# Pairwise bilinear products: a fixed issue order, units of one PSUM bank and a third product three units later

## Chip, core and metric

The kernel runs on one core of a Trainium2 chip. The metric is device time in microseconds, the median of several runs. The kernel before took 898.36 us (three runs, 897.13 to 898.63). A profiled execution of it spans 896.0 us.

## The reference

There are 32 fields of 128 numbers for each of 1024 rows, and one 128 x 128 matrix for each of the 496 pairs of fields. For each pair (i, j) with i < j, field i is multiplied by the pair's matrix, and the result element by element by field j, all in float32:

```python
FIELD_SIZE, EMBED_SIZE = 32, 128
_pairs = np.array(list(itertools.combinations(range(FIELD_SIZE), 2)))
v_i = inputs[:, I_IDX, :]            # inputs: (1024, 32, 128)
v_j = inputs[:, J_IDX, :]
transformed = jnp.einsum('bpd,ped->bpe', v_i, W)   # W: (496, 128, 128)
return transformed * v_j             # (1024, 496, 128)
```

The output has 1024 x 496 x 128 float32 numbers, 260 MB, and is much larger than the inputs.

## The kernel before

The host transposes the inputs, so that a field is a tile `x` of 128 x 1024 (embedding by rows of the batch) and the matrices come in chunks of four (`WC = 4`). Pairs are taken with falling i, so the first fields have few pairs: i = 30 has one, i = 29 two, and so on.

The first 15 pairs (`nq0`, "native") are multiplied as they are, in float32. For all others, each factor is split into three parts in a faster 32-bit format (float32r): `h` holds the leading part, `l` the rest, `d` a difference of the two. Then the product is the sum of three matrix products, where the sum of the first two is scaled by 1 + 2^-12 before the third is added:

```python
EPS = 2.0**-12
NATIVE = 5
LAG = 2
...
    def split_w(c):
        ...
        nc.scalar.mul(h, raw, 1.0 - 2.0**-13)                               # ACT
        nc.gpsimd.tensor_tensor(l, raw, h.bitcast(F32), ALU.subtract)       # POOL
        nc.gpsimd.tensor_scalar(hs, h.bitcast(F32), EPS, 1.0, ALU.mult, ALU.mult)
        nc.gpsimd.tensor_tensor(d, l.bitcast(F32), hs, ALU.subtract)
```

A field is split in the same way, in two halves of 512 columns. The main loop goes over whole pairs. Each pair has one PSUM tile `po` of 128 x 1024, two banks, of which there are four:

```python
    for q in range(NQ + LAG):
        if q < NQ:
            ...                       # loads; split of the chunk two ahead, split of the next field
            po[q] = ppool.tile([P, BT], F32, tag="po", name=f"po_{q}")
            ...
                for t in (0, 1):                        # first two products, L170
                    for h in range(0, BT, HB):
                        nc.tensor.matmul(po[q][:, h : h + HB], w_s[c][t][:, r],
                                         x_s[i][t][:, h : h + HB], start=t == 0, stop=t == 1)
                nc.scalar.mul(po[q], po[q], 1.0 + EPS)  # scaling in place, L177
        if q >= LAG:
            if q - LAG >= nq0:
                second(q - LAG)                         # third product, two matmuls, L135
            finish(q - LAG)                             # times field j (VectorE, L128), store
```

The kernel is written in a framework whose scheduler may put the instructions of an engine in another order than that of the source; here it is left to do so. All loads and stores are issued from SyncE's queue. Output tiles `ot` are 128 x 1024, six of them.

Of the kernel before, what the change touches and what calls it, by code (L numbers as in the profile page):

```python
# [1 line left out]

# [4 lines left out]

F32 = mybir.dt.float32
F32R = mybir.dt.float32r
ALU = mybir.AluOpType  # L10

P = 128
NF = 32
NQ = NF * (NF - 1) // 2
BT = 1024
HB = 512
WC = 4
EPS = 2.0**-12
NATIVE = 5
LAG = 2  # L20


def _pairs():

    return [(i, j) for i in range(NF - 2, -1, -1) for j in range(i + 1, NF)]


@with_exitstack
def kernel(
    ctx: ExitStack,  # L30
    tc: tile.TileContext,
    xt: bass.AP,
    wt: bass.AP,
    out: bass.AP,
):

    nc = tc.nc
    pairs = _pairs()
    nchunk = NQ // WC

    xpool = ctx.enter_context(tc.tile_pool(name="x", bufs=1))
    spool = ctx.enter_context(tc.tile_pool(name="xs", bufs=2))
    rpool = ctx.enter_context(tc.tile_pool(name="wr", bufs=4))
    wpool = ctx.enter_context(tc.tile_pool(name="ws", bufs=3))
    tpool = ctx.enter_context(tc.tile_pool(name="tmp", bufs=2))  # L60
    opool = ctx.enter_context(tc.tile_pool(name="o", bufs=6))
    ppool = ctx.enter_context(tc.tile_pool(name="ps", bufs=4, space=bass.MemoryType.PSUM))

    x_sb = {}

    def load_x(f, pieces=1):
        x_sb[f] = xpool.tile([P, BT], F32, tag=f"x{f}", name=f"x_{f}")
        s = BT // pieces
        for k in range(pieces):
            nc.sync.dma_start(out=x_sb[f][:, k * s : (k + 1) * s], in_=xt[:, f, k * s : (k + 1) * s])  # L70

    w_raw = {}

    def load_w(c, splits=(0, WC)):
        w_raw[c] = rpool.tile([P, WC, P], F32, tag="w", name=f"w_{c}")
        for a, b in zip(splits, splits[1:]):
            nc.sync.dma_start(out=w_raw[c][:, a:b, :], in_=wt[:, c * WC + a : c * WC + b, :])

    w_s = {}

    def split_w(c):

        raw = w_raw[c].rearrange("p q e -> p (q e)")
        h, l, d = [wpool.tile([P, WC * P], F32R, tag=t, name=f"{t}_{c}") for t in ("wh", "wl", "wd")]
        hs = tpool.tile([P, WC * P], F32, tag="t", name=f"whs_{c}")
        nc.scalar.mul(h, raw, 1.0 - 2.0**-13)  # L86
        nc.gpsimd.tensor_tensor(l, raw, h.bitcast(F32), ALU.subtract)  # L87
        nc.gpsimd.tensor_scalar(hs, h.bitcast(F32), EPS, 1.0, ALU.mult, ALU.mult)  # L88
        nc.gpsimd.tensor_tensor(d, l.bitcast(F32), hs, ALU.subtract)  # L89
        w_s[c] = (h, l, d)  # L90

    x_s = {}

    def split_x(f):

        h, l, d = [spool.tile([P, BT], F32R, tag=t, name=f"{t}_{f}") for t in ("xh", "xl", "xd")]
        for a in range(0, BT, HB):
            s = slice(a, a + HB)
            ls = tpool.tile([P, HB], F32, tag="t", name=f"xls_{f}_{a}")
            nc.scalar.mul(h[:, s], x_sb[f][:, s], 1.0 - 2.0**-13)  # L100
            nc.gpsimd.tensor_tensor(ls, x_sb[f][:, s], h[:, s].bitcast(F32), ALU.subtract)  # L101
            nc.gpsimd.tensor_scalar(l[:, s], ls, 1.0 / EPS, 1.0, ALU.mult, ALU.mult)  # L102
            nc.gpsimd.tensor_tensor(d[:, s], h[:, s].bitcast(F32), l[:, s].bitcast(F32), ALU.subtract)  # L103
        x_s[f] = (h, l, d)

    nq0 = NATIVE * (NATIVE + 1) // 2
    c0 = nq0 // WC

    load_w(0, (0, 1, WC))
    load_x(NF - 2, 2)  # L110
    load_x(NF - 1, 2)
    load_x(NF - 3)
    load_w(1)
    for f in (NF - 4, NF - 5):
        load_x(f)
    load_w(2)

    out_v = out.rearrange("q e b -> q e b")
    po = {}

    def finish(q):
        j = pairs[q][1]
        ot = opool.tile([P, BT], F32, tag="ot", name=f"ot_{q}")
        pieces = 2 if q >= NQ - 2 else 1
        s0 = BT // pieces
        for k in range(pieces):
            s = slice(k * s0, (k + 1) * s0)
            nc.vector.tensor_tensor(ot[:, s], po[q][:, s], x_sb[j][:, s], ALU.mult)  # L128
            nc.sync.dma_start(out=out_v[q, :, s], in_=ot[:, s])

    def second(q):
        i, _ = pairs[q]
        r = slice(q % WC * P, (q % WC + 1) * P)
        for h in range(0, BT, HB):
            nc.tensor.matmul(  # L135
                po[q][:, h : h + HB], w_s[q // WC][2][:, r], x_s[i][2][:, h : h + HB], start=False, stop=True,
                skip_group_check=True,
            )

    for q in range(NQ + LAG):  # L140
        if q < NQ:
            i, j = pairs[q]
            c = q // WC
            if q % WC == 0:
                if c + 3 < nchunk:
                    load_w(c + 3)
                for k in ([c + 2] if c > 0 else [0, 1, 2]):
                    if c0 <= k < nchunk:
                        split_w(k)
            if j == i + 1:  # L150
                for f in ([i - 4] if i < NF - 2 else [NF - 6]):
                    if f >= 0:
                        load_x(f)
                if 0 <= i - 1 < NF - 1 - NATIVE:
                    split_x(i - 1)
            po[q] = ppool.tile([P, BT], F32, tag="po", name=f"po_{q}")
            if q < nq0:
                for h in range(0, BT, HB):
                    nc.tensor.matmul(  # L159
                        po[q][:, h : h + HB],  # L160
                        w_raw[c][:, q % WC, :],
                        x_sb[i][:, h : h + HB],
                        start=True,
                        stop=True,
                    )
            else:
                r = slice(q % WC * P, (q % WC + 1) * P)
                for t in (0, 1):
                    for h in range(0, BT, HB):
                        nc.tensor.matmul(  # L170
                            po[q][:, h : h + HB],
                            w_s[c][t][:, r],
                            x_s[i][t][:, h : h + HB],
                            start=t == 0,
                            stop=t == 1,
                        )
                nc.scalar.mul(po[q], po[q], 1.0 + EPS)  # L177
        if q >= LAG:
            if q - LAG >= nq0:
                second(q - LAG)  # L180
            finish(q - LAG)


# [25 lines left out]
```

## Time and profile before

| Part | Value |
|---|---|
| Median time | 898.36 us |
| Span of the profiled execution | 896.0 us |
| Bytes moved | 310.03 MB, of them 260.05 MB written to HBM |
| VectorE multiply, 128 x 1024 (L128), 494 times | 1224 ns each |
| VectorE multiply, 128 x 512, 4 times | 685 ns each |
| ACT scaling in PSUM, 128 x 1024 (L177), 481 times | 1009 ns each |
| ACT split of a weight chunk, 128 x 512 (L86), 121 times | 624 ns each |
| GpSimd, one split of a chunk (L87, L88, L89) | 1277, 621 and 1294 ns |
| GpSimd, busy in all | 549.5 us |
| Matmuls of 512 columns, L170 and L135 | 4 and 2 for each split pair |
| Store of 512 KB, issue to landing | 3.8 us median |

PE is the matrix engine, PEld its weight loads (which overlap it), DVE is VectorE, ACT ScalarE, POOL GpSimd, SP SyncE. "L177" is line 177 of the kernel. In the page's busy shares, 100% would be an engine that never stands still. A matmul's recorded length is longer than the step from one to the next, since they are pipelined, so the steps between starts in the timeline say more. In a list of waits each line names who waited, for whom, how long in all, how often and the longest single wait.

### The profile page before, as it was taken

Reading aid. Unit: us, or ns where it says so; the run is one execution under the profiler, and the core shown is the slowest. Engines: PE = TensorE matmul, PEld = TensorE weight load, DVE = VectorE, ACT = ScalarE, POOL = GpSimd, SP = SyncE. Lnnn points to the kernel's source line nnn. Section 1 sums busy time; section 2 is a strip of 40 time slices with the busy share of each in tenths; the row PEclk is TensorE's granted clock in tenths of the full one; section 3 lists DMA queues with packets and bytes.
Section 4 is the critical chain, followed back from the end, with each engine's and each line's share of the span. In section 5 each row is a group of like instructions: output and inputs, shape, how many; then the busy total and the mean of one; then the engine's idle time right before and its main releaser. Section 6 shows DMA issues by size and latency. Waiting matters only on the chain.

```text
span 896.0 us, 10407 instructions
## 1 busy us (share of the span) xinstructions
PE 761.1 (85%) x2946; PEld 526.2 (59%) x2946; DVE 607.0 (68%) x498; ACT 558.2 (62%) x655; POOL 549.5 (61%) x523
## 2 busy tenths in 40 slices
PE   7988888888888888888888888888888888898887
PEld 2455555555666565555565666655656566665665
DVE  3666666666777666676676767776667777677766
ACT  2266666666676566566665667665756666666565
POOL 1878877777666774664747565665655647474441
PEclk9999999999999999999999999999999999999999
DMA  8999999899999898998998999998998899999997
GB/s 329 416 340 370 360 355 343 318 361 338 376 357 362 332 370 327 339 361 320 353 343 336 343 363 356 355 352 321 355 341 334 336 339 330 343 345 339 337 342 304
DMA packets 94666, 310.03 MB, mean 346 GB/s; under 512 B 10513, under 2 KB 10769, under 8 KB 94609
## 3 DMA queue, kind: packets, MB, share of 16 engines
q1 hardware_dynamic: 94608, 309.37, 92.3%
q8 instruction: 23, 0.38, 0.2%
q14 instruction: 35, 0.28, 0.1%
HBM read 49.28 MB, written 260.05 MB: 345 GB/s over the span
## 4 chain that ended last, share of the span: by engine, by line
PE 32%; ACT 25%; issue 19%; POOL 11%; DMA 1%; DVE 0%; POOLq 0%; ACTq 0%; DVEq 0%
ACT po L177 20%; PE po L170 17%; PE po L135 14%; ACT wh L86 4%; POOL wl L87 4%; POOL wd L89 4%; POOL whs L88 2%; DMA out_dram<-ot 1%; ACT xh L100 1%; POOL xls L101 1%; DVE ot L128 0%; POOL xl L102 0%; POOLq L87 0%; ACTq L177 0%; POOL xd L103 0%
## 5 line engine op out<-in xcount | busy, mean ns | idle before, releaser
L128 DVE TENSOR_TENSOR ot<-po,x 128x1024 f32<-128x1024 f32 (+1 forms) x498 | 607.0, 1220 | 285.4 <-ACT po L177 141.7
L177 ACT ACTIVATE po<-po 128x1024 f32<-128x1024 f32 x481 | 476.9, 1009 | 298.5 <-PE po L170 298.5
L135 PE MATMUL po<-xd,wd 128*128 128x512 f32 x962 | 325.7, 420 | 123.8 <-ACT po L177 123.0
L87 POOL TENSOR_TENSOR wl<-w,wh 128x512 fp32r<-128x512 f32 x121 | 154.5, 1277 | 301.7 <-ACT wh L86 301.7
L135 PEld LDWEIGHTS po<-xd,wd 128*128 128x128 f32 x962 | 152.7, 188 | 257.5 <-ACT po L177 162.8
L170 PE MATMUL po<-xh,wh 128*128 128x512 f32 x962 | 300.9, 394 | 0.0
L170 PE MATMUL po<-xl,wl 128*128 128x512 f32 x962 | 298.1, 391 | 0.0
L170 PEld LDWEIGHTS po<-xl,wl 128*128 128x128 f32 x962 | 180.6, 188 | 42.2
L170 PEld LDWEIGHTS po<-xh,wh 128*128 128x128 f32 x962 | 180.6, 188 | 42.1 <-issue 0.5
L89 POOL TENSOR_TENSOR wd<-wl,whs 128x512 fp32r<-128x512 f32 x121 | 156.6, 1294 | 7.9
L86 ACT ACTIVATE wh<-w 128x512 fp32r<-128x512 f32 x121 | 75.5, 624 | 19.3 <-DMA w<-in_wt_dram 19.3
L88 POOL TENSOR_SCALAR whs<-wh 128x512 f32<-128x512 f32 x121 | 75.1, 621 | 10.2
L101 POOL TENSOR_TENSOR xls<-x,xh 128x512 f32<-128x512 f32 x52 | 67.4, 1296 | 4.2
L103 POOL TENSOR_TENSOR xd<-xh,xl 128x512 fp32r<-128x512 f32 x52 | 66.9, 1287 | 2.2
L100 ACT ACTIVATE xh<-x 128x512 fp32r<-128x512 f32 x52 | 32.1, 621 | 13.6 <-PE po L170 8.7
L102 POOL TENSOR_SCALAR xl<-xls 128x512 fp32r<-128x512 f32 x52 | 32.4, 623 | 4.4
L159 PE MATMUL po<-x,w 128*128 128x512 f32 x60 | 29.6, 656 | 6.2 <-DMA x<-in_xt_dram 6.2
L159 PEld LDWEIGHTS po<-x,w 128*128 128x128 f32 x60 | 12.3, 209 | 22.6 <-issue 21.6
L86 ACT ACT_TABLE_LOAD x1 | 1.3, 1283 | 0.7 <-PEq L196 0.7
L196 POOL MEMSET const-float32-0.0<- 128x1 f32 x1 | 0.1, 99 | 0.2 <-issue 0.2
L196 POOL MEMSET const-bfloat16-1.0<- 128x1 bf16 x1 | 0.1, 102 | 0.0
L196 POOL MEMSET const-uint8-127<- 128x1 uint8 x1 | 0.1, 102 | 0.0
(1 smaller groups left out, 0.1 us busy)
## 6 DMA issues: line engine op xcount, KB each, us to landing
out_dram<-ot SPq DMA_DIRECT2D x494, 512.0 KB, 3.8
w<-in_wt_dram SPq DMA_DIRECT2D x123, 256.0 KB, 3.9
x<-in_xt_dram SPq DMA_DIRECT2D x30, 512.0 KB, 6.0
x<-in_xt_dram SPq DMA_DIRECT2D x4, 256.0 KB, 4.4
out_dram<-ot SPq DMA_DIRECT2D x4, 256.0 KB, 2.6
w<-in_wt_dram SPq DMA_DIRECT2D x1, 192.0 KB, 2.6
w<-in_wt_dram SPq DMA_DIRECT2D x1, 64.0 KB, 1.8
```

Source lines behind the costliest of these rows:

```text
L86: nc.scalar.mul(h, raw, 1.0 - 2.0**-13)
L87: nc.gpsimd.tensor_tensor(l, raw, h.bitcast(F32), ALU.subtract)
L88: nc.gpsimd.tensor_scalar(hs, h.bitcast(F32), EPS, 1.0, ALU.mult, ALU.mult)
L89: nc.gpsimd.tensor_tensor(d, l.bitcast(F32), hs, ALU.subtract)
L100: nc.scalar.mul(h[:, s], x_sb[f][:, s], 1.0 - 2.0**-13)
L101: nc.gpsimd.tensor_tensor(ls, x_sb[f][:, s], h[:, s].bitcast(F32), ALU.subtract)
L103: nc.gpsimd.tensor_tensor(d[:, s], h[:, s].bitcast(F32), l[:, s].bitcast(F32), ALU.subtract)
L128: nc.vector.tensor_tensor(ot[:, s], po[q][:, s], x_sb[j][:, s], ALU.mult)
L135: nc.tensor.matmul(po[q][:, h : h + HB], w_s[q // WC][2][:, r], x_s[i][2][:, h : h + HB], start=False, stop=True, skip_group_check=True,)
L159: nc.tensor.matmul(po[q][:, h : h + HB], w_raw[c][:, q % WC, :], x_sb[i][:, h : h + HB], start=True, stop=True,)
L170: nc.tensor.matmul(po[q][:, h : h + HB], w_s[c][t][:, r], x_s[i][t][:, h : h + HB], start=t == 0, stop=t == 1,)
L177: nc.scalar.mul(po[q], po[q], 1.0 + EPS)
```

## The change

The loop now goes over units of half a pair: 512 columns, one PSUM bank, eight such tiles instead of four of two banks. For each unit there are two matmuls, the scaling, and, three units later, the third product and the multiply. The third product thus stands three units behind its scaling, and this order is the one each engine gets: `tc.manual_schedule()` has the instructions issued as they are written. The splits go into a list with an earliest place and a deadline, and at most one is dealt out behind each pair, the most urgent first; a field's split is dealt out in two halves. Besides this, weight chunks are loaded four ahead instead of three (five tiles instead of four), output tiles go from six to five, and the first two fields are loaded from ScalarE's queue instead of SyncE's. The sizes of matmuls, splits and stores stay; scaling and multiply become twice as many of half the size. The aim is that the engines no longer wait for one another within a pair.

The core of the diff, with cuts marked:

```diff
-LAG = 2
+LAG = 3
+WLEAD = 4
+XLEAD = 3
...
-    rpool = ctx.enter_context(tc.tile_pool(name="wr", bufs=4))
+    rpool = ctx.enter_context(tc.tile_pool(name="wr", bufs=5))
...
-    opool = ctx.enter_context(tc.tile_pool(name="o", bufs=6))
-    ppool = ctx.enter_context(tc.tile_pool(name="ps", bufs=4, space=bass.MemoryType.PSUM))
+    opool = ctx.enter_context(tc.tile_pool(name="o", bufs=5))
+    ppool = ctx.enter_context(tc.tile_pool(name="ps", bufs=8, space=bass.MemoryType.PSUM))
...
+    todo = []
+    for c in range(c0, nchunk):
+        todo.append(((c - 2) * WC + 1, max(c * WC, nq0), lambda c=c: split_w(c)))
+    for i in range(NF - 2 - NATIVE, -1, -1):
+        for a in range(0, BT, HB):
+            todo.append((first_q[i + 1] + 1 if i < NF - 3 - NATIVE else 2, first_q[i], lambda i=i, a=a: split_x(i, a)))
+    todo.sort(key=lambda t: t[1])
...
-    load_x(NF - 2, 2)
-    load_x(NF - 1, 2)
+    load_x(NF - 2, 2, nc.scalar)
+    load_x(NF - 1, 2, nc.scalar)
...
+    ctx.enter_context(tc.manual_schedule())
...
+    def first(u):
+        q, h = divmod(u, 2)
+        ...
+        po[u] = ppool.tile([P, HB], F32, tag="po", name=f"po_{u}")
+        if q < nq0:
+            nc.tensor.matmul(po[u], w_raw[c][:, q % WC, :], x_sb[i][:, s], start=True, stop=True)
+        else:
+            for t in (0, 1):
+                nc.tensor.matmul(po[u], w_s[c][t][:, r], x_s[i][t][:, s], start=t == 0, stop=t == 1)
+            nc.scalar.mul(po[u], po[u], 1.0 + EPS)
+
+    def second(u):
+        ...
+        if q >= nq0:
+            nc.tensor.matmul(
+                po[u], w_s[q // WC][2][:, r], x_s[i][2][:, s], start=False, stop=True, skip_group_check=True
+            )
+        if h == 0:
+            ots[q] = opool.tile([P, BT], F32, tag="ot", name=f"ot_{q}")
+        nc.vector.tensor_tensor(ots[q][:, s], po.pop(u), x_sb[j][:, s], ALU.mult)
+        if q >= NQ - 2:
+            nc.sync.dma_start(out=out[q, :, s], in_=ots[q][:, s])
+        elif h == 1:
+            nc.sync.dma_start(out=out[q], in_=ots[q])
+
+    for u in range(2 * NQ + LAG):
+        q = u // 2
+        if u % (2 * WC) == 0 and q // WC + WLEAD < nchunk:
+            load_w(q // WC + WLEAD)
+        if u < 2 * NQ:
+            ...
+            first(u)
+        if u >= LAG:
+            second(u - LAG)
+        if u % 2 == 1:
+            ready = [t for t in todo if t[0] <= q]
+            if ready:
+                ready[0][2]()
+                todo.remove(ready[0])
```

## Prediction

> **What bounds the kernel now.** I began with busy shares, to see whether any engine is full, and with the transfers beside them (first and third part of the page, and the DMA rows of the slices).
>
> ```profile
> PE 761.1 (85%) x2946; PEld 526.2 (59%) x2946; DVE 607.0 (68%) x498; ACT 558.2 (62%) x655; POOL 549.5 (61%) x523
> DMA  8999999899999898998998999998998899999997
> GB/s 329 416 340 370 360 355 343 318 361 338 376 357 362 332 370 327 339 361 320 353 343 336 343 363 356 355 352 321 355 341 334 336 339 330 343 345 339 337 342 304
> ...
> q1 hardware_dynamic: 94608, 309.37, 92.3%
> ```
>
> No engine is full, yet the DMA engines look nearly so, at 346 GB/s on average. Two things say that they are not the limit. One slice moved 416 GB/s. And the view of the DMA queue's waits has its stores waiting for VectorE ("SPq L129 <- DVE ot L128: 574.6"), while in the view of the engines' waits no store delays VectorE. I then asked for short windows. The columns are: length, busy time and count of PE, PEld, DVE, ACT and POOL, clock, DMA share, GB/s.
>
> ```profile
> 16.00:46.00 30.00, 28.27 (x80) 14.52 (x79) 20.46 (x18) 8.95 (x12) 22.98 (x24) 1.00 1.03 417
> 400.00:428.00 28.00, 24.11 (x95) 16.49 (x95) 18.42 (x16) 18.80 (x23) 14.59 (x15) 1.00 0.88 322
> 429.00:444.00 15.00, 12.30 (x50) 8.49 (x48) 10.48 (x9) 8.71 (x10) 13.28 (x13) 1.00 1.03 407
> 410.00:412.00 2.00, 2.00 (x10) 1.45 (x9) 1.85 (x2) 1.51 (x3) 0.00 (x0) 1.00 0.27 109
> ```
>
> Where work is always queued, DMA sustains 407 to 417 GB/s; in between it runs dry (410 to 412 us: 27%, 109 GB/s). So the stores wait for the computation. Next, who waits there (engine and line, releaser, total us, times, longest):
>
> ```profile
> ACT po L177 <- PE po L170: 298.5, 237, 7.8
> PEld po L135 <- ACT po L177: 162.8, 195, 1.7
> DVE ot L128 <- ACT po L177: 141.7, 89, 1.6
> PE po L135 <- ACT po L177: 123.0, 245, 1.2
> DVE ot L128 <- PE po L135: 114.7, 347, 1.7
> ```
>
> PE and ACT wait for each other. The timeline shows the form (start, length, engine, operation, idle before it):
>
> ```profile
> 403.26 0.62 PE L170 MATMUL po<-xh,wh 128*128 128x512 f32 x2
> 403.72 0.61 PE L170 MATMUL po<-xl,wl 128*128 128x512 f32 x2
> 404.52 0.73 PE L135 MATMUL po<-xd,wd 128*128 128x512 f32 x2 [0.19 <-ACT po L177]
> 405.97 0.74 PE L135 MATMUL po<-xd,wd 128*128 128x512 f32 x2 [0.72 <-ACT po L177]
> ```
> ```profile
> 403.46 1.01 ACT L177 ACTIVATE po<-po 128x1024 f32<-128x1024 f32 x1 [1.75 <-PE po L170]
> 404.38 0.62 ACT L86 ACTIVATE wh<-w 128x512 fp32r<-128x512 f32 x1
> 404.91 1.02 ACT L177 ACTIVATE po<-po 128x1024 f32<-128x1024 f32 x1
> ...
> 411.41 0.62 ACT L86 ACTIVATE wh<-w 128x512 fp32r<-128x512 f32 x1
> ```
>
> PE issues the first two products of two pairs back to back. ACT scales the first pair from 403.46 to 404.47, and PE's third product starts at 404.52, right behind it. ACT then splits a weight chunk before it scales the second pair, and PE stands another 0.72 us. The scheduler has put the pairs so that the lag of two written in the source is hardly there. The chunk splits recur every 411.41 - 404.38 = 7.03 us, which is 4 pairs: **1.76 us per pair**. Over the whole body I get the same: VectorE's product of pair 15 ends near 37 us (timeline), the last near 892, so (892 - 37) / 481 = 1.78 us.
>
> **What the Trainium skill says.** "PSUM — Partial Sum Buffer", section "PSUM bank collisions raise a hardware error", has engines kept apart bank by bank. A tile of two banks is therefore handed over as a whole, as the trace has it: one ACT instruction of 1024 columns, and both third products behind it. "Perfetto Trace Analysis", section "Optimizing Scalar/DVE Operations", says that larger operations help a saturated engine, while breaking them up can help where an engine that is not saturated causes bubbles in others; ACT at 62% with 123.0 us of PE waiting is that case. It puts the cost of one more instruction on PSUM at about 125 ns for DVE and 51 ns for ScalarE; the trace agrees roughly for DVE (146 ns of recorded time, below). "TensorE: Matmul & The Clock Gate", section "Back-to-back issue gap", has N/2.4 + 2.5 ns, so 216 ns for 512 columns; here two take 403.72 - 403.26 = 0.46 us, 230 ns each. "HBM Reference", section "Specifications (TRN2)", has about 425 GB/s for a core that streams alone; 417 was measured here.
>
> **The change part by part**, per pair, the 481 split pairs first.
>
> - **PE.** The same six matmuls: 6 x 0.23 = 1.38 us. A third product comes three half-pair units later. A unit is 0.69 us of PE work, and between the first two products of u and its third lie the third products of u-3, u-2 and u-1 and the first two of u+1, u+2 and u+3: 9 matmuls, 2.07 us. The scaling needs about 0.6, or 1.2 with a split ahead of it. So the 123.0 us of waiting should nearly vanish; alone this would make 896 - 123 = 773.
> - **ACT.** 962 scalings of 512 columns for 481 of 1024. No such row exists. It must cost over half of 1009 ns, and at most the 624 ns of the 512-column split: 1.01 to 1.25 us per pair, plus (75.5 + 32.1) / 481 = 0.22 of splits, so 1.23 to 1.47. Two consecutive 1024s take 1.93 us and not 2.02, as records overlap; I take 1.3.
> - **VectorE.** 992 halves for 498. The four halves at the end took 685 ns each, so 1.37 us per pair against 1.22, 73 us more in sum, with nothing of it on the path while below PE.
> - **GpSimd.** 549.5 / 481 = 1.14 us, unchanged. One split takes 1277 + 621 + 1294 = 3.19 us. For a field of n pairs it needs 2 + n/4 splits, 6.4 + 0.8n. With 1.5n available, it is late only for n of 6, 7 and 8: about 2, 1.5 and 1 us. A cost of up to 5 us.
> - **PSUM.** Eight tiles of one bank are the same memory as four of two. A unit lives through two matmuls, scaling, third product and multiply, some 4 units; 8 are there.
> - **Transfers.** The same 310.03 MB. Output tiles fall from 6 to 5. One is filled in 1.4 us and landed 3.8 us after issue, so 5.2 us of holding is covered by 5 x 1.5 = 7.5 us. First loads of two fields go out from ACT's queue; under 1 us. Looking further ahead in loads costs nothing.
> - **The first 15 pairs** have one matmul per half, with PE nearly full (28.27 of 30 us). They stay: 37 us to the end of pair 15.
>
> So computation can run at 1.4 us per pair, and **the transfers become the bound**: 310.03 MB / 0.407 to 0.417 = 743 to 762 us, plus about 2 us until the first loads and 4 for the last store, 750 to 768. They won't be perfectly full, since computation has only some 8% in hand over the 310.03 / 496 / 0.412 = 1.52 us of a pair. Every time a cluster of splits or a boundary lets the queue run dry, full speed is lost for a moment. I allow 25 to 35 us, which means a mean of about 392 GB/s: 791, plus 2 to 3 us between the span and the given time (898.36 against 896.0). **794 us.**
>
> **Rivals.**
>
> - **A. The transfers are the bound already.** For it: nines in nearly every slice. 309.37 MB at a 92.3% share is 374 GB/s when busy, which would give 310.03 / 0.374 + 6 = 835 us. Against it: 407 and 417 GB/s in full stretches. I chose the upper rate because the low rates stand beside dry spells; that rests on a few stretches, so 835 stays in my range.
> - **B. The fixed order makes new stalls.** No engine can now step past a late input, and a split on ACT stands ahead of scalings. For it: splits come in threes where a field starts. Against it: the third product has near 0.9 to 1.4 us to spare, and 8 banks. Half the PE waiting kept would give 896 - 62 = 834 or so.
> - **C. Smaller instructions make ACT or VectorE the bound.** If ACT took 624 ns, 1.47 us x 481 + 37 + 5 = 749, still under the transfers. It could only make them less full.
> - **D. Slower.** It would need more than 1.80 us per pair. No engine's sum is near it.
>
> **Range and chances.** The lower end is the full rate, 768. The upper end is A or B alone, 835. Over 880 would need both at once. So 768 to 836, with 0.95 for faster by over 2%, 0.04 for within, 0.01 for slower.
>
> **What the profile after would show.** Right: PE's wait for ACT at the third product near zero; a mean of 385 GB/s or more, with slices over 400 in the middle; VectorE halves of about 685 ns and a VectorE share over 80%; waits of VectorE or its output tile for stores appearing, since stores now lag. Wrong by A: DMA share near 1.0 with 375 GB/s. Wrong by B: PE or VectorE still idle behind ACT or GpSimd, and dry spells of DMA. Wrong on ACT: scalings of 512 columns over 624 ns.

## The result and the profile after

The changed kernel takes **780.49 us** (779.83 to 781.02) against 898.5: a ratio of 0.869, 95% interval 0.867 to 0.870. The prediction was 794, with a range of 768 to 836. A profiled execution spans 779.2 us. First the page's busy shares, the slices' rows of DMA, its queue, and the shares of the chain that ended last:

```profile
PE 725.1 (93%) x2946; PEld 544.4 (70%) x2946; DVE 632.7 (81%) x992; ACT 622.3 (80%) x1136; POOL 549.9 (71%) x523
DMA  9899999999999999999999999999999999999998
GB/s 341 352 397 399 411 403 400 405 399 411 395 411 403 399 401 412 401 399 407 394 408 410 399 390 388 411 408 410 397 403 401 392 403 403 404 393 407 402 408 341
...
q1 hardware_dynamic: 94032, 308.32, 100.3%
...
DMA 42%; PE 31%; DVE 12%; POOL 8%; issue 4%; SPq 1%; DVEq 0%; POOLq 0%
```

Away from the edges the same bytes now flow at 388 to 412 GB/s in each slice; in the kernel before it was 318 to 376. Transfers lead the chain with 42%, of which stores are 41%. Before, the same line read:

```profile
PE 32%; ACT 25%; issue 19%; POOL 11%; DMA 1%; DVE 0%; POOLq 0%; ACTq 0%; DVEq 0%
```

The window that held the dry spells before (columns as in the prediction), and the whole of the body:

```profile
400.00:428.00 28.00, 26.82 (x112) 20.42 (x111) 23.91 (x38) 23.55 (x44) 20.89 (x20) 1.00 1.02 407
46.00:770.00 724.00, 686.25 (x2844) 525.28 (x2845) 606.28 (x951) 607.90 (x1112) 524.66 (x495) 1.00 1.02 403
```

The waits have turned round:

```profile
PEld po L147 <- DVE ot L161: 93.2, 135, 2.5
...
DVE ot L161 <- DMA out_dram<-ot: 67.7, 75, 3.2
DVE ot L161 <- PE po L156: 44.8, 60, 1.9
...
PEld po L156 <- ACT po L148: 0.4, 1, 0.4
```

At the third product PE had waited 123.0 us for the scaling and its weight load 162.8 us; PE's wait is gone and the weight load's is 0.4 us. Instead VectorE waits for output tiles that stores still hold (67.7), and PE for PSUM that VectorE holds (34.2, its weight load 93.2). The delay comes from the stores backwards, where it came from PE and ACT forwards. That the queue of stores waits for VectorE tells nothing by itself: it did so for 574.6 us before, and still does for 365.8 us ("SPq L165 <- DVE ot L161: 365.8"). VectorE's wait for stores is what is new. The timeline of PE shows the pace in between:

```profile
400.01 0.39 PE L147 MATMUL po<-xl,wl 128*128 128x512 f32 x1
400.23 0.39 PE L156 MATMUL po<-xd,wd 128*128 128x512 f32 x1
400.46 0.40 PE L147 MATMUL po<-xh,wh 128*128 128x512 f32 x1
400.70 0.40 PE L147 MATMUL po<-xl,wl 128*128 128x512 f32 x1
400.93 0.40 PE L156 MATMUL po<-xd,wd 128*128 128x512 f32 x1
```

In this stretch a third product starts every 400.93 - 400.23 = 0.70 us without a gap. Two rows of part 5 give the halved instructions:

```profile
L161 DVE TENSOR_TENSOR ot<-po,x 128x512 f32<-128x512 f32 x992 | 632.7, 686 | 140.7 <-DMA out_dram<-ot 67.7
L148 ACT ACTIVATE po<-po 128x512 f32<-128x512 f32 x962 | 544.4, 580 | 130.1 <-PE po L147 77.3
```

### The profile page after: what moved, and what is told of

Same layout as the page of the kernel before. It is cut to its first block, busy times and chain, and to the rows that moved or that the text cites. A ratio compares the mean times of both kernels' runs of the same rounds, so it can differ in the third digit from the quotient of the medians.

```text
span 779.2 us, 11845 instructions
## 1 busy us (share of the span) xinstructions
PE 725.1 (93%) x2946; PEld 544.4 (70%) x2946; DVE 632.7 (81%) x992; ACT 622.3 (80%) x1136; POOL 549.9 (71%) x523
## 2 busy tenths in 40 slices
DMA packets 94676, 310.12 MB, mean 398 GB/s; under 512 B 10512, under 2 KB 10768, under 8 KB 94608
## 4 chain that ended last, share of the span: by engine, by line
DMA 42%; PE 31%; DVE 12%; POOL 8%; issue 4%; SPq 1%; DVEq 0%; POOLq 0%
DMA out_dram<-ot 41%; PE po L147 22%; DVE ot L161 12%; PE po L156 10%; POOL wd L91 2%; POOL wl L89 2%; POOL whs L90 1%; POOL xls L104 1%; DMA x<-in_xt_dram 1%; DMA w<-in_wt_dram 1%; SPq L79 1%; SPq L165 0%; POOL xd L106 0%; POOL xl L105 0%; DVEq L161 0%
## 5 line engine op out<-in xcount | busy, mean ns | idle before, releaser
L161 DVE TENSOR_TENSOR ot<-po,x 128x512 f32<-128x512 f32 x992 | 632.7, 686 | 140.7 <-DMA out_dram<-ot 67.7
L148 ACT ACTIVATE po<-po 128x512 f32<-128x512 f32 x962 | 544.4, 580 | 130.1 <-PE po L147 77.3
L147 PE MATMUL po<-xh,wh 128*128 128x512 f32 x962 | 391.5, 407 | 39.5 <-DVE ot L161 34.2
L147 PE MATMUL po<-xl,wl 128*128 128x512 f32 x962 | 377.8, 393 | 1.5 <-POOL wl L89 1.5
L156 PE MATMUL po<-xd,wd 128*128 128x512 f32 x962 | 377.3, 393 | 0.0
L147 PEld LDWEIGHTS po<-xh,wh 128*128 128x128 f32 x962 | 181.0, 188 | 133.6 <-DVE ot L161 93.2
L89 POOL TENSOR_TENSOR wl<-w,wh 128x512 fp32r<-128x512 f32 x121 | 156.1, 1290 | 156.3 <-ACT wh L88 153.8
L156 PEld LDWEIGHTS po<-xd,wd 128*128 128x128 f32 x962 | 181.2, 188 | 40.3 <-ACT po L148 0.4
L103 ACT ACTIVATE xh<-x 128x512 fp32r<-128x512 f32 x52 | 32.6, 629 | 13.6 <-DMA x<-in_xt_dram 13.5
```

Source lines behind the costliest of these rows:

```text
L103: nc.scalar.mul(h, x_sb[f][:, s], 1.0 - 2.0**-13)
L147: nc.tensor.matmul(po[u], w_s[c][t][:, r], x_s[i][t][:, s], start=t == 0, stop=t == 1)
L148: nc.scalar.mul(po[u], po[u], 1.0 + EPS)
L156: nc.tensor.matmul(po[u], w_s[q // WC][2][:, r], x_s[i][2][:, s], start=False, stop=True, skip_group_check=True)
L161: nc.vector.tensor_tensor(ots[q][:, s], po.pop(u), x_sb[j][:, s], ALU.mult)
```

## The experiments

The change does three things at once: it fixes the order, halves the units, and deals the splits out. I took them apart, then asked what bounds the result. For the reading it helps to count, in the compiled order of PE's instructions, how many matmuls lie between a unit's first two products and its third. Those matmuls are all that the scaling has to hide behind. (The trace does not number the tiles; third products are taken in the order of their units.)

```
kernel           unit      matmuls between (times)              in us at 0.23 each
before           pair      0 (11), 2 (114), 4 (114), 6 (242)    0 to 1.38
changed          half      9 (956 of 962)                       2.07
free_order       half      1 (129), 2 (139), 3 (679), other 15  mostly 0.69
before_fixed     pair      12 (477 of 481)                      2.76
```

The source of the kernel before says two pairs, which would be 12. No third product got that.

### The order alone, and the small units alone

before_fixed is the kernel before with one line more; free_order is the changed kernel with that line out:

```diff
 # before_fixed (in the kernel before)
+    ctx.enter_context(tc.manual_schedule())
 # free_order (in the changed kernel)
-    ctx.enter_context(tc.manual_schedule())
```

The letters in the expectations from here on are not those of the prediction: O is the theory that the fixed order brings the gain, B that units of one bank do, S that dealing out the splits does.

> The kernel before with its order fixed as written and nothing else: whole pairs, two banks, third product two pairs later, splits in clumps at the start of a chunk and of a field. Theory O: 785 to 815 us, PE waiting for ACT at the third product under 20 us, DMA near 400 GB/s. Rival B (one-bank units): 860 us or more. Rival S (splits must be dealt out): 830 to 870 us, with PE behind ACT or GpSimd where splits come in clumps.

Measured: **783.08 us**, ratio 0.872 (0.870 to 0.874). One line gives nearly all of the gain, with clumped splits and whole pairs left as they were. The page and the waits:

```profile
PE 763.0 (98%) x2946; PEld 517.8 (66%) x2946; DVE 607.4 (78%) x498; ACT 563.3 (72%) x655; POOL 550.4 (70%) x523
...
DMA packets 94665, 310.03 MB, mean 396 GB/s; under 512 B 10512, under 2 KB 10768, under 8 KB 94608
```
```profile
PEld po L171 <- DVE ot L129: 127.3, 410, 0.4
...
PE po L136 <- ACT po L178: 5.3, 9, 1.6
```

The third product's wait for ACT is 5.3 us. What is left is the weight load of PE waiting about 0.3 us in most pairs for VectorE to give back a tile of two banks. Rivals B and S both fall, as far as the total time goes.

> The changed kernel without the line that fixes the order; the scheduler then puts the third product one unit behind its first two for 818 of 962 units and directly behind for 134. Theory O (the fixed order, which keeps the third product far behind the scaling, brings the gain): most of the gain is lost, 830 to 890 us, PE waiting for ACT at the third product more than 80 us. Rival B (units of one bank bring the gain, since halves are handed over sooner): 780 to 800 us, hardly any such wait.

Measured: **960.96 us**, ratio 1.071 (1.068 to 1.073): half-pair units and dealt splits, in an order of the scheduler's choosing, are slower than the kernel before. It is also above the 830 to 890 us that were expected. The waits, the largest first:

```profile
PEld po L155 <- ACT po L147: 365.2, 812, 1.1
...
ACT po L147 <- PE po L146: 266.2, 442, 10.4
DVE ot L160 <- PE po L155: 250.5, 580, 1.6
PE po L155 <- ACT po L147: 82.6, 269, 0.7
```

PE's weight load for the third product waits 812 times for the scaling. Halved units halve the distance that one unit of lag is worth. The distances account for most of the time: lag1 below, with 3 matmuls between for nearly every unit, takes 847 us, and here 129 units have two matmuls less (0.46 us) and 139 one less (0.23 us), which gives 847 + 59 + 32 = 938 of the 961 us. This is an estimate made after the runs.

### How far apart is enough

Next the distance was set, with the order fixed. First in half-pair units, LAG = 1 and LAG = 2 instead of 3:

> The changed kernel with the third product one unit later instead of three. Between the first two products and the third of a unit lie 3 matmuls, 0.69 us; the scaling needs 0.58 us and a split ahead of it another 0.62. Theory O: each of 173 splits delays PE by about 0.6 us and scaling by itself is just at the edge, so 810 to 860 us. Rival (distance does not matter once order is fixed and units are one bank): 780 to 785 us.

Measured: 846.67 us, ratio 0.943 (0.941 to 0.945), as theory O had it. The wait for the scaling at the third product is back:

```profile
PEld po L156 <- ACT po L148: 192.7, 579, 0.5
```

> The third product two units later. 6 matmuls, 1.38 us, against 1.2 us of scaling with one split ahead. Theory O: 780 to 785 us, as for three, since one split is just covered and small delays are hidden behind the transfers. Rival (every unit of distance counts): 790 to 820 us.

Measured: 778.21 us, ratio 0.867 (0.865 to 0.869), within 0.3% of three units. 1.38 us of distance covers scaling and one split (0.58 + 0.62 = 1.20); the weight load's wait for the scaling is 3.4 us, in 15 places.

Then in whole pairs, LAG = 1 and LAG = 0 in before_fixed:

> The kernel before with fixed order and the third product one whole pair later. In the order that the scheduler gave the kernel before, 356 third products stand one pair later and 125 directly behind their own first two. Theory Z (the products without distance are what cost): between first and third products lie 6 matmuls, 1.38 us, against 1.01 of scaling, so only the splits in clumps hurt, 785 to 820 us. Rival (one pair is already too near, the scheduler's other choices included): 870 us or more.

Measured: 803.60 us, ratio 0.897 (0.894 to 0.899), as theory Z had it; this leaves out a fourth run, of 818.21 us, in which the granted clock was 0.977 instead of 0.989 to 0.993.

```profile
ACT wh L86 <- DMA w<-in_wt_dram: 82.5, 61, 12.2
...
PE po L136 <- ACT po L178: 61.1, 74, 3.2
```

Here the wait is not that of the lengths added up in the expectation. In 61 places ACT, whose order is fixed too, stands at the split of a weight chunk that has not landed, with a scaling behind it; 54.0 of PE's 61.1 us follow such a place within 3.5 us. The changed kernel loads chunks four ahead instead of three, and ACT waits 2.1 us for them. In before_fixed ACT waits even longer for them, 129.6 us, but the 12 matmuls between hide it.

> The same with no distance: the third product directly behind its pair's first two. Theory Z: each pair takes 4 matmuls, the scaling and 2 matmuls one after the other, 0.92 + 1.01 + about 0.1 + 0.46 = 2.5 us, so 1180 to 1260 us. A mix of 356 pairs at the pace of whole_lag1 and 125 at this pace should then give the kernel before within 25 us of its 898. Rival: the mix misses by more than 50 us.

Measured: 1373.97 us, ratio 1.533 (1.530 to 1.536); I had expected at most 1260.

```profile
DVE ot L129 <- PE po L136: 742.9, 480, 1.8
...
PE po L136 <- ACT po L178: 538.9, 481, 1.4
```

PE waits at each of 481 pairs, 538.9 / 481 = 1.12 us, and VectorE waits in turn for PE's late products.

The mix that I had expected misses: 804 + 125/481 x (1374 - 804) = 952 against 898. That is 54 us off, beyond the 25 us of theory Z and also beyond the 50 us from which the rival was to hold. The count above shows one reason. I had counted 125 pairs of the kernel before as having no distance, but 114 of them have another pair's third product in between, 0.46 us. Putting 1.12 us on 11 pairs, 0.66 on 114, and 0.20 on the 114 with four matmuls gives 12 + 75 + 23 = 110, so 804 + 110 = 914. That is within 2% of 898, but it was worked out after the result, and the rest stays open. That whole_lag0 is 0.27 us per pair slower than my sum can be read from its trace, as a mean over the 481 pairs: 1.12 us from a pair's first matmul to the start of its scaling where I had put 0.92, since the scaling starts 0.43 us after the start of the last of the four matmuls and not one step of 0.23; 1.01 for the scaling; 0.08 until the third product; and 0.57 from there to the next pair where I had put 0.46. Together 2.78 us. The trend over all runs is clear in one table:

```
matmuls between    0      3 (halves)   6 (halves)   6 (pairs)   9 (halves)   12 (pairs)
us              1374        847           778          804         780          783
```

At six, pairs cost more than halves. A pair's scaling takes 1.01 us of the 1.38 and a half's 0.58, so a split ahead of it (0.62) fits only with halves; but the waits of whole_lag1 show that most of its loss comes from the late weight chunks.

### Dealing the splits out

```diff
-            if ready:
-                ready[0][2]()
-                todo.remove(ready[0])
+            if q % WC == 1:
+                for t in ready:
+                    t[2]()
+                    todo.remove(t)
```

> The changed kernel with all splits that are ready issued at once behind the second pair of each chunk, instead of one behind each pair. Three splits in a row put 1.87 us ahead of the scaling, against 1.4 us of spare distance, at each of 25 fields; theory O: under 1 us of PE waiting per clump, hidden behind transfers, so 778 to 792 us. Rival S (dealing out is needed): 800 us or more, with PE waiting for ACT at the third product over 25 us.

Measured: 777.84 us, ratio 0.866 (0.865 to 0.868). PE's weight load waits 4.8 us for the scaling, in 12 places. Dealing out brings nothing here. This version is even some 2 us faster than the changed kernel (777.84, 776.26 to 778.35, against 779.71, 779.60 to 781.44, on the same chip); the reason shows below, at early_split.

### What bounds it now

half_store stores half of the columns and computes all; half_store_before does the same in before_fixed; no_third leaves the third product out, and with it a third of PE's work on those pairs:

```diff
 # half_store
-            nc.sync.dma_start(out=out[q], in_=ots[q])
+            nc.sync.dma_start(out=out[q, :, :HB], in_=ots[q][:, :HB])
 # no_third
-        if q >= nq0:
+        if q < 0:
             nc.tensor.matmul(po[u], w_s[q // WC][2][:, r], ...
```

> The changed kernel storing only the first 512 of 1024 columns of each pair (half of the output is left unwritten; all is still computed), 180 MB instead of 310. Theory T (the transfers bound the changed kernel): the time falls to what PE needs, 36 us to the first split pair and 962 units of 0.69 us, so 700 to 730 us. Rival (computation still bounds it): 770 us or more.

Measured: 706.22 us, ratio 0.787 (0.785 to 0.789). PE and VectorE are now nearly full (page, part 1):

```profile
PE 686.4 (97%) x2946; PEld 553.8 (79%) x2946; DVE 671.3 (95%) x992; ACT 613.6 (87%) x1136; POOL 551.4 (78%) x523
```

> The changed kernel without the third product (left out, so the sum lacks its last part); PE has 4 matmuls per pair instead of 6, 219 us less of work. Theory T (transfers bound): 770 to 783 us, nothing or little gained. Rival (PE bounds): 700 us or less.

Measured: 775.04 us, ratio 0.863 (0.861 to 0.865). With 219 us less PE work the kernel gains some 5 us, while half of the store bytes were worth 74. So **the transfers bound the changed kernel**, with only a small share for PE.

> The kernel before with fixed order, storing half of the columns as in half_store. It shows what the one-bank units are worth once transfers no longer hide it. With four tiles of two banks a tile comes free only after a multiply of 1.22 us that starts when both third products are done, about 1.45 us after the slot in which the next user wants it begins to count down from 1.38 us; I expect 1.46 to 1.55 us per pair, so 740 to 785 us, against 700 to 730 for the changed kernel. Rival (one-bank units bring nothing even in computation): within 1% of half_store.

Measured: 771.54 us, ratio 0.860 (0.858 to 0.861). Here is what the small units do:

```profile
PE 758.9 (99%) x2946; PEld 518.5 (67%) x2946; DVE 607.4 (79%) x498; ACT 574.2 (75%) x655; POOL 551.5 (72%) x523
```
```profile
PEld po L172 <- DVE ot L129: 131.1, 432, 0.4
```

With half of the stores gone, before_fixed becomes only 12 us shorter, since PE's weight load waits 0.3 us for a two-bank tile in 432 pairs whatever the stores do; the changed kernel becomes 74 us shorter, and in half_store the same wait is nearly gone:

```profile
PEld po L147 <- DVE ot L161: 2.7, 3, 1.2
```

The changed kernel's structure is thus worth 771.54 - 706.22 = 65 us of computation, or (769.5 - 37) / 481 = 1.52 us per pair against (704.2 - 36) / 481 = 1.39, and the transfers hide it nearly all. The two also differ in dealing, loads ahead and output tiles, but the only long wait of PE that goes away is the one for two-bank tiles. By its recorded PE share before_fixed looks fuller than the changed kernel (98% against 93%). A matmul's record, 395 ns in the median there, is longer than the step of 230 ns, so short pauses between starts don't show as idle time.

### A version that beats both

In the changed kernel DMA has one dry spell of about 3 us, near the first split pairs. The timeline around it (GpSimd's first split, then the chunk that the second split pair needs, and PE):

```profile
18.10 1.27 POOL L104 TENSOR_TENSOR xls<-x,xh 128x512 f32<-128x512 f32 x1 [17.66 <-ACT xh L103]
...
34.55 1.26 POOL L89 TENSOR_TENSOR wl<-w,wh 128x512 fp32r<-128x512 f32 x1
...
35.87 0.50 PE L147 MATMUL po<-xl,wl 128*128 128x512 f32 x1 [1.51 <-POOL wl L89]
```

PE stands at the first products of the second split pair until their chunk is split, with the third products of the first pair queued behind them. GpSimd works without a pause from 18.10 us on; it starts so late because its first split is of a field that has not arrived ("ACT xh L103 <- DMA x<-in_xt_dram: 13.5"). early_split uses the distance of two, deals the first chunk out earlier, and loads one more field at the start:

```diff
-LAG = 3
-XLEAD = 3
+LAG = 2
+XLEAD = 4
...
-        todo.append(((c - 2) * WC + 1, max(c * WC, nq0), lambda c=c: split_w(c)))
+        todo.append(((c - 2) * WC + 1 if c > c0 else 2, max(c * WC, nq0), lambda c=c: split_w(c)))
```

> The changed kernel with third products two units later, the first needed weight chunk split ahead of the second field, and one more field loaded at the start. In the changed kernel DMA stands idle for about 3 us near 34 to 37 us, since the first split pair waits for GpSimd, which has split half a field too many by then (3.19 us). Removing that should give back about 3 us: 775 to 778 us. If the gap has another cause, 778 to 781 us.

> The changed kernel itself, on the same chip as early_split and before it in nothing: 779 to 782 us.

Measured, on one chip: 777.10 us, ratio 0.866 (0.865 to 0.867), and 779.71 us for the changed kernel, ratio 0.869 (0.868 to 0.870). The window 34 to 37 us, changed kernel first, then early_split:

```profile
34.00:37.00 3.00, 1.49 (x7) 0.96 (x6) 2.18 (x4) 1.37 (x4) 2.83 (x4) 1.00 0.18 55
```
```profile
34.00:37.00 3.00, 2.51 (x9) 1.54 (x10) 1.81 (x4) 1.78 (x4) 2.83 (x4) 1.00 1.01 412
```

The dry spell is gone, and the kernel gains 2.6 us of the 3 that it held, 0.3%. The cause that I had expected was not it: in both kernels five splits stand ahead of that chunk. But GpSimd starts them 1.2 us earlier, with a chunk that is there:

```profile
16.90 1.27 POOL L89 TENSOR_TENSOR wl<-w,wh 128x512 fp32r<-128x512 f32 x1 [16.45 <-ACT wh L88]
...
33.36 1.28 POOL L89 TENSOR_TENSOR wl<-w,wh 128x512 fp32r<-128x512 f32 x1
```

Three small edits were made together. Two earlier runs narrow down which of them counts. lag2, with the distance of two alone, keeps part of the dry spell (DMA share 0.52 in 34 to 37 us). clumped has neither the distance of two nor the additional field, but its first split too is of a chunk that is there, at 15.10 us, and its window has no dry spell:

```profile
34.00:37.00 3.00, 2.03 (x9) 1.27 (x8) 1.74 (x4) 1.45 (x4) 2.83 (x4) 1.00 0.97 375
```

Its time, 776.26 to 778.35 us on the same chip, can't be told from early_split's 776.40 to 777.81. So the other two edits are not needed to remove the dry spell, and that they add anything is not shown.

## Why the prediction was right, step by step

- **What bounds the kernel before: right.** Computation in an unfavourable order did, not the transfers. One line that fixes the order took 898 to 783, and with the order fixed the time follows the distance of the third product.
- **PE: right.** The waiting for ACT went from 123.0 us to nothing, that of the weight load from 162.8 to 0.4. The change gives 2.07 us of distance, where I had put the need at 1.2 with a split ahead; lag2 shows that 1.38 is enough. The pace of 1.4 us per pair came out at 1.39 in half_store. There matmuls in float32r start 227 ns apart; each native one of the first 15 pairs stands in the trace as two instructions (60 for 30 matmuls) that start 429 ns apart. In "Back-to-back issue gap" I had taken the figure for a single matmul, 216 ns, which is near; the same section of the Trainium skill's "TensorE: Matmul & The Clock Gate" puts the sustained spacing for 512 columns at about 131 ns, and nothing here comes near that.
- **ACT and VectorE: right.** 580 and 686 ns against at most 624 and 685. With splits ACT has 2 x 0.58 + 0.22 = 1.38 us per pair in recorded time, just above my 1.3. VectorE was not quite off the path, as I had put it: it makes up 12% of the chain. My reading of the skill's cost of one more instruction was loose: "Optimizing Scalar/DVE Operations" in "Perfetto Trace Analysis" gives its 125 and 51 ns as busy times and puts the recorded latency at about double, so the 146 ns should not have been set beside 125. In steps from start to start, where nothing waits, the second instruction costs 2 x 608 - 1141 = 75 ns on VectorE and 2 x 515 - 921 = 109 ns on ACT; in recorded time it is 148 and 151 ns. VectorE's is lower than that section has it and ACT's higher.
- **The transfers become the bound: right**, shown by half_store and no_third. Their rate was 398 GB/s on average, where I had taken 392. Two terms of that sum were mis-sized, in opposite directions. The sustained rate was 403 GB/s and not 407 to 417, so the floor was 310.12 / 0.403 + 6 = 776 us where I had 750 to 768. For dry spells I allowed 25 to 35 us, and there was one of about 3 us. The second error is the larger, so the sum came out 14 us too long; that it came so near is in part luck. The term for output tiles was thin as well: a store took 5.8 us to land and not 3.8, so a tile is held for 7.2 us of the 7.5 that five tiles cover, and VectorE waited 67.7 us in 75 places. Whether a sixth tile would give some of it back was not run.
- **Rival A: refuted.** The low rates of the kernel before came with its dry spells; the same traffic runs at 400 GB/s when it is kept queued.
- **Rival B: no.** The fixed order makes no new stalls of weight: PE's weight loads wait 2.1 us for GpSimd in all. **Rival C: no**, by the row of 580 ns.
- **GpSimd: half right.** I expected up to 5 us in the fields of 6, 7 and 8 pairs, from GpSimd's pace. The loss found, 3 us, was at the first split pairs, which are in the field of 6, and came from GpSimd's late start; in the fields of 7 and 8 PE has no wait for GpSimd of over 0.2 us.
- **What I didn't say:** which part carries the gain. I credited distance, small units and dealing together. The runs show that the line which fixes the order carries it, that small units are worth some 65 us of computation, which the transfers hide, and that dealing is worth nothing measurable. In particular I had taken breaking up ACT's instructions to be the remedy for PE's waiting; free_order has them broken up and is 62 us slower than the kernel before.

## What to carry to other kernels

A distance written into a loop is worth only what the issued order keeps of it: count the instructions between producer and consumer in the order that was compiled, multiply by the pace, and compare with what must fit in between, here 1.38 us against a scaling and one split, 1.20 us. In a fixed order, ask also what can be late in front of the producer: ACT's waits for weight chunks were hidden with 12 matmuls between (129.6 us of ACT's, 5.3 of PE's) and not with 6 (82.5 and 61.1). Before halving units, fix that; smaller units in an order with little distance were slower than large ones (961 against 898 us). A transfer share of 92% need not mean a bound: look for dry spells, and for whether computation waits for stores. That stores wait for computation was so in both kernels.

## What was not expected of the hardware

In runs whose queue runs dry, more packets are slow. In the trace's packet records a packet of 4096 bytes takes 159 ns in the median in both kernels, but 6.2% took over 200 ns in the kernel before and 1.9% in the changed one; the means are 171 and 163 ns. In the kernel before, 59% of the slow packets start within three microseconds of the end of a dry spell (a stretch in which the engines were less than half busy), against 32% of all packets of this size; in 16 to 46 us, which has no dry spell, 0.5% are slow. So the busy share contains time of this kind, and the rate read from it, 374 GB/s when busy, understated what the engines could do: the changed kernel sustained 403. The next chunk's load often falls in the same place. Away from the first 50 and last 20 us, 18.8% of the packets that run beside a packet of such a load are slow in the kernel before and 2.8% in the changed one; of the others it is 4.3% and 1.2%. The difference between the kernels is thus there with and without a load beside; what slows a packet is not shown.
